# Layer 0 of a four-layer convolution stack: paired products summed in PSUM by TensorE, frame transforms dealt anew over the slots

## The chip, the cores and the metric

The kernel runs on one core of one Trainium2 chip. The metric is the device time of one execution in microseconds (us), the median of three runs where several were made.

## The reference, cut to what matters

The input x has the shape (4, 16, 512, 512): four images of sixteen frames. Four layers follow, each of the form x = x + f(groupnorm(x)). Only layer 0 is touched here:

```
def _denoise_block(x, w1, b1, w2, b2, w3, b3, a, b, c):
    trip = _triplets(x)                  # frame t with its two neighbours t-1, t+1 (mirrored at the ends)
    ...
    o = a * conv5x5(trip, w1, dilation 1) + b * conv5x5(trip, w2, dilation 2) + c * conv5x5(trip, w3, dilation 4)
    return tanh(o + biases)
y = _denoise_block(groupnorm(x), block 1)
z = _denoise_block(y, block 2)
x = x + z
```

All in float32. Layer 1 is a quantised 3x3 convolution, layer 2 a 17x17 box filter, layer 3 a product in Fourier space. They are the same in both kernels.

## The kernel before, in words

**Groups and slots.** Layer 0 runs its two blocks one after the other (`conv` 0, then `conv` 1), for 4 images each. The text calls them the first and the second convolution. Along the frame axis the three-tap sum over t-1, t, t+1 is computed for four output frames at a time out of six products in place of twelve (a short-convolution scheme, F(4,3)). Four output frames are a *group*: 4 groups an image, 16 in the first convolution (groups 0 to 15), 16 in the second (16 to 31). A group has six *slots*, p = 0 to 5, one for each product; `ORDER` says which product q runs in which slot. One slot is 144 float32 matmul instructions of TensorE (288 matmul records), 80 that write 64 output rows and 64 that write 32, all on one transformed frame `v[q]` and one set of weights `w[q]`. They write a PSUM tile `m` of 128 x 4 x 512; there are two such tiles.

**Before the products: frame transforms.** A group has six input frames d0 to d5, each a tile of 128 x 2376 (ten such tiles in a free list, `self.free`). VectorE makes from them, with one instruction of 128 x 2376 for each step, the six transformed frames: v1 and v2 from d1 to d4, v3, v4, v5 and v0. `early` does v1 and v2 (and v0) in the group before, `late` does the rest in the group's own slots 0 to 2. A group shares d0 and d1 with the group before (its d4 and d5), so it fetches four frames, one in each of the slots 0, 1, 2 and 4 of the group before (`fetch`); the first group of an image fetches five, in slots 0 to 4.
In the first convolution a frame is made from x: ScalarE normalises (L412), VectorE transposes (L445). In the second it is read from a scratch tensor y in DRAM (`y_frame`): 14 DMAs on SyncE's queue, then six small edge instructions on ScalarE (`mirror`, L484 to L488) and one small addition on VectorE (`added`, L492) in the slot after.

**After the products: gather.** In the slot after a product, `gather` takes its PSUM tile. With m1 ... the products, the four output frames are y0 = m0+m1+m2+m3+m4, y1 = (m1-m2)+2(m3-m4), y2 = (m1+m2)+4(m3+m4), y3 = (m1-m2)+8(m3-m4)+m5. Before the change ScalarE copies m1 to a tile A and m3 to C (L637); VectorE makes B = A-m2, A = A+m2, D = C-m4, C = C+m4 (L641, L642), then E = 4C+A in two halves (output frame 2), A = A+C (L648), A = A+m0 (L651), C = 2D+B, B = 8D+B, B = B+m5. ScalarE takes the tanh of each (L665 in the second convolution, L672 in the first). There is one buffer for E: the second half waits for the tanh of the first.

**What sets the order.** The whole of layer 0 stands in one order written out by hand (`slot`): each engine runs its own instructions in this order and waits on semaphores. Within a slot the order is: products; gather of the product before; tanh of A, B or C; edges; `late`; rows (the sums and extremes of finished frames: L695 and L698 on VectorE); the output (transposes `zr`, L689); the rest, in which frames are made or `added`; `early` for the next group; `fetch`. The transfers of a slot stand at its end on SyncE's queue: frames first, then the loads of x (`xb`), then the stores of finished frames (`x<-xb`); each also waits for a place in the slot's matmuls, so that they are spread over it. ScalarE also does the sums of finished frames (L714), in the same buffer as E.

**What a product waits for.** The matmuls of slot p need their transformed frame, and the PSUM tile to be free: the tile of slot p is that of slot p-2, so the gather of slot p-2, which runs during slot p-1, must be done with it.

Of the kernel before, what the change touches and what calls it, by code (L numbers as in the profile page):

```python
# [13 lines left out]
F32 = mybir.dt.float32  # L14
# [6 lines left out]
P = 128  # L21
# [7 lines left out]
PX = 32  # L29
# [6 lines left out]
ORDER = (1, 2, 3, 4, 0, 5)  # L36
# [86 lines left out]
class Layer0:  # L123
# [407 lines left out]
    def early(self, gr, step):  # L531

        nc, d, v = self.nc, gr["d"], gr["v"]
        if step == 0:
            v[1] = self.free.pop(0)
            self.stt(v[1], d[2], -4.0, d[4])
            return
        e, f = v[1], self.free.pop(0)
        self.stt(f, d[1], -4.0, d[3])
        nc.vector.tensor_add(e, e, f)  # L540
        self.stt(f, f, -2.0, e)
        v[2] = f
        if gr["g"] > 0:
            self.stt(d[0], d[0], 4.0, d[4])
            self.stt(d[0], d[2], -5.0, d[0])
            v[0] = d[0]

    def late(self, gr, p):
        nc, d, g = self.nc, gr["d"], gr["g"]
        if p == 0:  # L550
            o = d[2]
            if g == 0:
                o = gr["v"][0] = self.free.pop(0)
            nc.vector.tensor_sub(o, d[4], d[2])
            nc.vector.tensor_sub(d[1], d[3], d[1])
            gr["o"] = o
        elif p == 1:
            self.stt(d[2], d[1], 2.0, gr["o"])
            gr["v"][3] = d[2]
            if g == 3:  # L560
                self.free.append(d[4])
                nc.vector.tensor_scalar_mul(d[3], d[1], -4.0)
            else:
                nc.vector.tensor_sub(d[3], d[5], d[3])
                self.stt(d[3], d[1], -4.0, d[3])
            gr["v"][5] = d[3]
        elif p == 2:
            self.stt(d[1], d[1], -4.0, d[2])
            gr["v"][4] = d[1]


    def products(self, gr, p):
        nc, conv, q = self.nc, gr["conv"], ORDER[p]
        ps = self.psum.tile([P, 4, 512], F32, name=f"m{self.now}", tag="m")
# [15 lines left out]
        def product(at, i, weights, d, e, j, n):  # L590
            nc_ = 8 if conv else 16
            return nc.tensor.matmul(  # L592
                ps[at, i, :].rearrange("p (k c m) -> p k c m", k=nc_, c=2),
                w[PX * i : PX * i + PX, weights],
                source(i, d, e, j),
                start=(n == 0),
                stop=(n == len(order) - 1),
                skip_group_check=True,
            )
# [15 lines left out]
        gr["m"][q] = ps  # L615

    def gather(self, gr, p):

        nc, conv = self.nc, gr["conv"]
        m = gr["m"].pop(ORDER[p])  # L620
# [14 lines left out]
        if p in (0, 2):  # L635
            t = s["A" if p == 0 else "C"] = new("A" if p == 0 else "C")
            nc.scalar.copy(of(t), m)  # L637
        elif p in (1, 3):
            o, t = ("B", "A") if p == 1 else ("D", "C")
            s[o] = new(o)  # L640
            nc.vector.tensor_sub(of(s[o]), of(s[t]), m)  # L641
            nc.vector.tensor_add(of(s[t]), of(s[t]), m)  # L642
            if p == 3:
                for h in range(2):
                    e = new("E")
                    self.stt(e, s["C"][:, h], 4.0, s["A"][:, h])
                    self.activated(gr, 2, h, e)
                nc.vector.tensor_add(flat("A"), flat("A"), flat("C"))  # L648
        else:
            t = s["A" if p == 4 else "B"]  # L650
            nc.vector.tensor_add(of(t), of(t), m)  # L651
            if p == 4:
                self.stt(flat("C"), flat("D"), 2.0, flat("B"))
                self.stt(flat("B"), flat("D"), 8.0, flat("B"))
# [75 lines left out]
    def slot(self, n, p):  # L730
# [48 lines left out]
        if nxt:  # L779
            step = p - (3 if nxt["g"] == 0 else 2)  # L780
            if step in (0, 1):
                self.early(nxt, step)
            self.fetch(nxt, p)
# [1014 lines left out]
```

## Time and profile before

| | us |
|---|---|
| median of 3 runs | 5003.81 (4993.23 to 5010.5) |
| the profiled execution, device time | 5009.29 |
| its span, first to last instruction | 5007.5 |
| around the span | 1.8 |
| mean granted TensorE clock | 0.977 |
| products of layer 0 (L592), first to last | 63 to 2785 |

TensorE is busy for 94% of the span, VectorE for 80%, ScalarE for 51%. Layer 0 fills the first 2785 us. The page has a row for each engine's busy time, a chain of waits that is followed back from the last instruction, and groups of instructions by line with their mean duration; the trace behind it gives the same for any stretch. Engines are named PE (TensorE), DVE (VectorE), ACT (ScalarE), POOL (GpSimd), SP or SPq (SyncE's queue). L592 is line 592 of the kernel; L500 is a helper (`stt`) that stands for every scalar-tensor-tensor instruction of layer 0, so such rows are told apart by their tiles.

### The profile page before, as it was taken

The page shows a single profiled execution, that of the slowest core. Times are in us where ns is not written, and L with a number is a line of the kernel's source. Part 1 is how long each engine was busy: PE and PEld are TensorE (multiplying, and loading weights), DVE is VectorE, ACT ScalarE, POOL GpSimd, SP SyncE. Part 2 cuts the span into 40 slices and gives each one's busy share as a digit, 9 for nine tenths or more (in the row PEclk, how much of TensorE's full clock was granted, in tenths as well). Part 3 has the DMA queues.
Part 4 walks back from the last instruction along what each step waited for, and adds up shares of the span by engine and source line. Part 5 has one row for each costly group of instructions (what it writes and reads, how often), then busy time and mean ns, then how long its engine had stood idle before and what let it go on. Part 6 is the DMA issues. An engine that isn't in the chain of part 4 may idle for free.

```text
span 5007.5 us, 200506 instructions
## 1 busy us (share of the span) xinstructions
PE 4718.3 (94%) x90224; PEld 2669.6 (53%) x90224; DVE 4028.1 (80%) x4031; ACT 2558.2 (51%) x4156; POOL 21.4 (0%) x90
## 2 busy tenths in 40 slices
PE   4899999999999999989989699989999989999999
PEld 1344444444444444434434345548888767777776
DVE  8888888979779899899899666655555588888887
ACT  3465656563324443444434555545444456666665
POOL 0000000000000000000000000000000000000000
PEclk9999999999999999999999899999999999999999
DMA  5656665563577677776875688866666655555553
GB/s 174 167 159 168 173 167 158 154 177 99 120 143 157 151 158 158 155 161 145 163 151 134 171 267 271 266 227 228 215 215 203 208 137 148 149 143 141 152 147 115
DMA packets 393819, 850.64 MB, mean 170 GB/s; under 512 B 70912, under 2 KB 86400, under 8 KB 384512
## 3 DMA queue, kind: packets, MB, share of 16 engines
q1 hardware_dynamic: 385456, 827.22, 61.9%
q8 instruction: 707, 11.58, 1.1%
q10 hardware_dynamic: 7504, 10.60, 0.8%
q14 instruction: 152, 1.25, 0.1%
HBM read 497.51 MB, written 340.03 MB: 167 GB/s over the span
## 4 chain that ended last, share of the span: by engine, by line
PE 79%; DVE 12%; DMA 3%; issue 3%; ACT 2%; SPq 1%; ACTq 0%; POOL 0%; DVEq 0%; POOLq 0%
PE m L592 41%; PE l1p L1052 10%; PE l2p L1159 8%; PE u L1627 5%; PE s L1568 5%; PE u L1568 4%; DVE frame L500 3%; PE u L1590 2%; PE pt L1602 2%; DVE l2o L1199 2%; PE l2p L1210 1%; DVE frame L445 1%; DVE st L1200 1%; DMA frame<-y 1%; DVE B L641 1%
## 5 line engine op out<-in xcount | busy, mean ns | idle before, releaser
L592 PE MATMUL m<-frame,l0w 32*64 32x512 f32 (+1 forms) x55296 | 2609.5, 611 | 176.1 <-DVE frame L540 63.3
L592 PEld LDWEIGHTS m<-frame,l0w 32*64 32x64 f32 (+1 forms) x55296 | 1178.6, 119 | 1606.0 <-issue 1389.4
L500 DVE SCALAR_TENSOR_TENSOR frame<-frame,frame 128x2376 f32<-128x2376 f32 x232 | 607.9, 2629 | 8.6
L1052 PE MATMUL l1p<-l1q,l_wt 32*32 32x512 f32 (+1 forms) x9216 | 429.6, 604 | 48.0 <-DVE l1q L1039 41.5
L1199 DVE TENSOR_TENSOR l2o<-l2x,l2p 128x512 f32<-128x512 f32 x256 | 172.8, 675 | 263.6 <-PE l2p L1159 263.6
L714 ACT ACTIVATE junk<-xb,neg 128x1024 f32<-128x1024 f32 x256 | 294.1, 1149 | 85.4 <-issue 42.6
L1052 PEld LDWEIGHTS l1p<-l1q,l_wt 32*32 32x32 f32 (+1 forms) x9216 | 189.9, 113 | 249.8 <-issue 209.5
L1159 PEld LDWEIGHTS l2p<-k_c_band,l2y 128*128 128x128 f32 x2048 | 256.7, 190 | 75.8 <-issue 55.0
L1188 ACT COPY l2y<-l2p 128x512 f32<-128x512 f32 x256 | 150.0, 586 | 280.7 <-PE l2p L1159 280.7
L1159 PE MATMUL l2p<-k_c_band,l2y 128*128 128x144 f32 (+1 forms) x2048 | 284.2, 292 | 6.1
L445 DVE STREAM_TRANSPOSE frame<-xp 128x1056 f32<-128x1056 f32 x128 | 261.2, 2124 | 29.7 <-ACT xp L414 29.7
L1159 PE MATMUL l2p<-k_c_band,l2n 128*128 128x144 f32 (+1 forms) x2048 | 266.6, 290 | 13.8 <-DMA l2x<-x 6.8
L1159 PEld LDWEIGHTS l2p<-k_c_band,l2n 128*128 128x128 f32 x2048 | 260.1, 195 | 14.5 <-ACT l2n L1177 12.2
L1627 PE MATMUL u<-k_c_hil,zt 128*128 128x128 f32 x2048 | 255.9, 278 | 0.0
L1627 PEld LDWEIGHTS u<-k_c_hil,zt 128*128 128x128 f32 x2048 | 238.4, 192 | 2.1 <-issue 0.8
L1603 ACT COPY zt<-pt 128x512 f32<-128x512 f32 x256 | 131.4, 599 | 208.2 <-PE pt L1602 208.2
L1533 DVE TENSOR_TENSOR xc<-l3n,k_c_tab 128x2048 f32<-128x2048 f32 x64 | 146.7, 2293 | 107.6 <-ACT l3n L1517 107.6
L1067 ACT ACTIVATE l1o<-l1p,k_l_bias,l_osc 128x1024 f32<-128x1024 f32 x128 | 147.2, 1201 | 144.8 <-PE l1p L1052 139.3
L1646 DVE SCALAR_TENSOR_TENSOR l3o<-u,l3t 128x256 f32<-128x256 f32 x512 | 192.5, 427 | 22.3 <-ACT l3t L1638 19.5
L1069 DVE BATCH_NORM_STATS2 l1st<-l1o 128x6 f32<-128x512 f32 x256 | 158.2, 681 | 54.4 <-ACT l1o L1067 54.2
L1052 PE MATMUL l1p<-l1x,l_wt 32*32 32x512 f32 (+1 forms) x3064 | 195.0, 593 | 0.0
L1033 ACT ACTIVATE l1t<-l1x,l1own,l1own 128x1024 f32<-128x1024 f32 x128 | 151.8, 1234 | 81.4 <-DMA l1x<-x 76.5
(313 smaller groups left out, 6256.7 us busy)
## 6 DMA issues: line engine op xcount, KB each, us to landing
y<-y SPq DMA_DIRECT2D x256, 264.0 KB
xb<-in_x SPq DMA_DIRECT2D x512, 128.0 KB
x<-l1o SPq DMA_DIRECT2D x256, 256.0 KB
l2x<-x SPq DMA_DIRECT2D x64, 1024.0 KB
x<-l2o SPq DMA_DIRECT2D x64, 1024.0 KB
l3x<-x SPq DMA_DIRECT2D x256, 256.0 KB
out<-l3o SPq DMA_DIRECT2D x256, 256.0 KB
l1x<-x SPq DMA_DIRECT2D x252, 256.0 KB
```

The source lines that it names most:

```text
L445: nc.vector.transpose(v[:, :, :, h, 1:17].rearrange("p k u m -> p k m u"), xp)
L500: self.nc.vector.scalar_tensor_tensor(o, x, f, y, ALU.mult, ALU.add)
L592: return nc.tensor.matmul(ps[at, i, :].rearrange("p (k c m) -> p k c m", k=nc_, c=2), w[PX * i : PX * i + PX, weights], source(i, d, e, j) ...
L714: nc.scalar.activation(junk, xs[:, h], f, bias=neg, accum_out=self.out_sums[b][n][:, 2 * t + h : 2 * t + h + 1])
L1033: nc.scalar.activation(t[:, at], x[:, at], AF.Identity, bias=own[1], scale=own[0])
L1052: ins = nc.tensor.matmul(ps[at : at + hi - lo, b, :], wt[rows, d, lo:hi], qs[v % 3][rows, k, d : d + W] if d < 3 else raws[v][rows, k], st ...
L1069: nc.vector.bn_stats(st[b][:, u, :], o[:, b, :])
L1159: nc.tensor.matmul(ps[:, lo:hi], lhs[:, k, at : at + P], band[:, j : j + hi - lo], start=(k == 0), stop=(k == 3), skip_group_check=True,)
L1199: nc.vector.tensor_add(o[:, hb, :], xt[:, hb, :], ps)
L1568: nc.tensor.matmul(ps[b][32 * j : 32 * j + 32], f[rows, n, j, :], x[rows, j, :], start=(i == 0), stop=(i == 2 and tag == "s"), skip_group_ ...
L1627: nc.tensor.matmul(po[:, bass.ts(k, P)], zt[:, b, k ^ 1, :], hil[:, k, :], start=False, stop=(k == 3), skip_group_check=True,)
L1646: nc.vector.scalar_tensor_tensor(o[:, v].rearrange("p k u -> p u k"), po[:, HW:W].rearrange("p (u k) -> p u k", u=2), s, t.rearrange("p (u ...
```

## The change

In `ORDER` products 2 and 3 change places: 1, 3, 2, 4, 0, 5. A group takes two PSUM tiles for its six products and keeps them: slots 0, 2 and 4 write the first, slots 1, 3 and 5 the second. The matmuls of slots 2 (product 2), 3 (product 4) and 4 (product 0) no longer start their tile anew but add to what is in it; product 5 starts anew. So the tiles hold m1, then m1+m2, then m1+m2+m0; and m3, then m3+m4, then m5.

`gather` follows. ScalarE takes 2 m1 and 2 m3 in place of the plain copies, and two more copies, of m1+m2 (over A) and of m3+m4 (over C). VectorE takes B = A-m and D = C-m as before, reads m3+m4 for the two halves of E from PSUM in place of C, and makes A = C+m in one step in slot 4's gather. Three instructions of 128 x 2048 on VectorE go: A = A+m, C = C+m, A = A+C.

The frame transforms are the same instructions, given letters and dealt to slots by two tables, `AHEAD` (in the group before) and `SINCE` (in the group itself). The letters: a and f start v1 and v2, s finishes v1, t finishes v2; z and Z make v0; o and e are two differences; 3, u5 and 4 make v3, v5 and v4.

```diff
@@ -33,7 +33,9 @@
 ALONE = (((-4, 4), (6, 0)), ((-1, 6), (3, 5)))
 NPB = 2 * len(DELTA)
 NQ = 6
-ORDER = (1, 2, 3, 4, 0, 5)
+ORDER = (1, 3, 2, 4, 0, 5)
+AHEAD = {0: {3: "ao", 4: "fse"}, 1: ({2: "az", 3: "fs", 4: "Zoe"}, {2: "az", 3: "fstZ", 4: "oe"})}
+SINCE = {0: ({0: "3t", 1: "u5", 2: "4"}, {0: "3t", 1: "u5", 2: "4"}), 1: ({0: "3t", 1: "u5", 2: "4"}, {0: "3", 1: "u5", 2: "4"})}
 KN = 9 * 264
 NFRAMES = 10
 AFTER = mybir.DependencyInfo(mybir.DependencyClass.Sync, mybir.DependencyReason.SCHED_ONLY)
@@ -528,50 +530,62 @@
         if held is not None:
             self.free.append(held)
 
-    def early(self, gr, step):
-
-        nc, d, v = self.nc, gr["d"], gr["v"]
-        if step == 0:
-            v[1] = self.free.pop(0)
-            self.stt(v[1], d[2], -4.0, d[4])
-            return
-        e, f = v[1], self.free.pop(0)
-        self.stt(f, d[1], -4.0, d[3])
-        nc.vector.tensor_add(e, e, f)
-        self.stt(f, f, -2.0, e)
-        v[2] = f
-        if gr["g"] > 0:
-            self.stt(d[0], d[0], 4.0, d[4])
-            self.stt(d[0], d[2], -5.0, d[0])
-            v[0] = d[0]
+    def early(self, gr, p):
+        plan = AHEAD[1][gr["conv"]] if gr["g"] else AHEAD[0]
+        self.transform(gr, plan.get(p, ""))
 
     def late(self, gr, p):
-        nc, d, g = self.nc, gr["d"], gr["g"]
-        if p == 0:
-            o = d[2]
-            if g == 0:
-                o = gr["v"][0] = self.free.pop(0)
-            nc.vector.tensor_sub(o, d[4], d[2])
-            nc.vector.tensor_sub(d[1], d[3], d[1])
-            gr["o"] = o
-        elif p == 1:
-            self.stt(d[2], d[1], 2.0, gr["o"])
-            gr["v"][3] = d[2]
-            if g == 3:
-                self.free.append(d[4])
-                nc.vector.tensor_scalar_mul(d[3], d[1], -4.0)
-            else:
-                nc.vector.tensor_sub(d[3], d[5], d[3])
-                self.stt(d[3], d[1], -4.0, d[3])
-            gr["v"][5] = d[3]
-        elif p == 2:
-            self.stt(d[1], d[1], -4.0, d[2])
-            gr["v"][4] = d[1]
+        self.transform(gr, SINCE[gr["g"] > 0][gr["conv"]].get(p, ""))
+
+    def transform(self, gr, steps):
+
+        nc, d, v, g = self.nc, gr["d"], gr["v"], gr["g"]
+        for step in steps:
+            if step == "a":
+                v[1] = self.free.pop(0)
+                self.stt(v[1], d[2], -4.0, d[4])
+            elif step == "z":
+                self.stt(d[0], d[0], 4.0, d[4])
+            elif step == "Z":
+                self.stt(d[0], d[2], -5.0, d[0])
+                v[0] = d[0]
+            elif step == "f":
+                v[2] = self.free.pop(0)
+                self.stt(v[2], d[1], -4.0, d[3])
+            elif step == "s":
+                nc.vector.tensor_add(v[1], v[1], v[2])
+            elif step == "t":
+                self.stt(v[2], v[2], -2.0, v[1])
+            elif step == "o":
+                gr["o"] = d[2]
+                if g == 0:
+                    gr["o"] = v[0] = self.free.pop(0)
+                nc.vector.tensor_sub(gr["o"], d[4], d[2])
+            elif step == "e":
+                nc.vector.tensor_sub(d[1], d[3], d[1])
+            elif step == "3":
+                self.stt(d[2], d[1], 2.0, gr["o"])
+                v[3] = d[2]
+            elif step == "u":
+                if g < 3:
+                    nc.vector.tensor_sub(d[3], d[5], d[3])
+            elif step == "5":
+                if g == 3:
+                    self.free.append(d[4])
+                    nc.vector.tensor_scalar_mul(d[3], d[1], -4.0)
+                else:
+                    self.stt(d[3], d[1], -4.0, d[3])
+                v[5] = d[3]
+            elif step == "4":
+                self.stt(d[1], d[1], -4.0, d[2])
+                v[4] = d[1]
 
 
     def products(self, gr, p):
         nc, conv, q = self.nc, gr["conv"], ORDER[p]
-        ps = self.psum.tile([P, 4, 512], F32, name=f"m{self.now}", tag="m")
+        if p < 2:
+            gr["m"][p] = self.psum.tile([P, 4, 512], F32, name=f"m{self.now}", tag="m")
+        ps = gr["m"][p % 2]
         v = gr["v"][q]
         w = self.w[q]
         runs = [(e, pair) for e in range(2) for pair in PAIRS], [(e, two) for e in range(2) for two in ALONE]
@@ -593,7 +607,7 @@
                 ps[at, i, :].rearrange("p (k c m) -> p k c m", k=nc_, c=2),
                 w[PX * i : PX * i + PX, weights],
                 source(i, d, e, j),
-                start=(n == 0),
+                start=(n == 0 and q in (1, 3, 5)),
                 stop=(n == len(order) - 1),
                 skip_group_check=True,
             )
@@ -612,12 +626,11 @@
                         out = slice(64 * j + PX * u, 64 * j + PX * u + PX)
                         ins = product(out, i, slice(at, at + PX), d, e, j, n)
             self.marks.append(ins.ins)
-        gr["m"][q] = ps
 
     def gather(self, gr, p):
 
         nc, conv = self.nc, gr["conv"]
-        m = gr["m"].pop(ORDER[p])
+        m = gr["m"][p % 2]
         s = gr.setdefault("s", {})
 
         def new(tag):
@@ -632,26 +645,29 @@
         def flat(t):
             return s[t].rearrange("p h n -> p (h n)")
 
-        if p in (0, 2):
-            t = s["A" if p == 0 else "C"] = new("A" if p == 0 else "C")
-            nc.scalar.copy(of(t), m)
-        elif p in (1, 3):
-            o, t = ("B", "A") if p == 1 else ("D", "C")
-            s[o] = new(o)
-            nc.vector.tensor_sub(of(s[o]), of(s[t]), m)
-            nc.vector.tensor_add(of(s[t]), of(s[t]), m)
+        if p < 2:
+            t = s["AC"[p]] = new("AC"[p])
+            nc.scalar.mul(of(t), m, 2.0)
+        elif p < 4:
+            t = s["AC"[p - 2]]
+            o = s["BD"[p - 2]] = new("BD"[p - 2])
+            nc.vector.tensor_sub(of(o), of(t), m)
             if p == 3:
                 for h in range(2):
                     e = new("E")
-                    self.stt(e, s["C"][:, h], 4.0, s["A"][:, h])
+                    half = slice(1024 * h, 1024 * h + 1024)
+                    if conv:
+                        self.stt(e.rearrange("p (k r) -> p k r", r=PX), m[:, h], 4.0, of(s["A"])[:, h])
+                    else:
+                        self.stt(e, m[:, half], 4.0, of(s["A"])[:, half])
                     self.activated(gr, 2, h, e)
-                nc.vector.tensor_add(flat("A"), flat("A"), flat("C"))
+            nc.scalar.copy(of(t), m)
+        elif p == 4:
+            nc.vector.tensor_add(of(s["A"]), of(s["C"]), m)
+            self.stt(flat("C"), flat("D"), 2.0, flat("B"))
+            self.stt(flat("B"), flat("D"), 8.0, flat("B"))
         else:
-            t = s["A" if p == 4 else "B"]
-            nc.vector.tensor_add(of(t), of(t), m)
-            if p == 4:
-                self.stt(flat("C"), flat("D"), 2.0, flat("B"))
-                self.stt(flat("B"), flat("D"), 8.0, flat("B"))
+            nc.vector.tensor_add(of(s["B"]), of(s["B"]), m)
 
 
     def activated(self, gr, i, h, src):
@@ -777,9 +793,7 @@
         self.do("rest")
         self.do("last")
         if nxt:
-            step = p - (3 if nxt["g"] == 0 else 2)
-            if step in (0, 1):
-                self.early(nxt, step)
+            self.early(nxt, p)
             self.fetch(nxt, p)
         if cur and cur["conv"] == 0 and cur["b"] + 1 < B and p >= 2:
             self.input_stats(cur["b"] + 1, 4 * cur["g"] + p - 2)
```

## The prediction

> **What bounds the kernel now.** I read the page first: its busy times, and the chain of waits by engine.
>
> ```profile
> PE 4718.3 (94%) x90224; PEld 2669.6 (53%) x90224; DVE 4028.1 (80%) x4031; ACT 2558.2 (51%) x4156; POOL 21.4 (0%) x90
> ...
> PE 79%; DVE 12%; DMA 3%; issue 3%; ACT 2%; SPq 1%; ACTq 0%; POOL 0%; DVEq 0%; POOLq 0%
> ```
>
> TensorE bounds the program, and the DVE share of the chain is what a change could take out. Only layer 0 changes, so next come the stretches of its two convolutions.
>
> ```profile
> 63.00:1414.00 1351.00, 1297.01 (x27648) 591.53 (x27656) 1151.42 (x793) 686.74 (x1137) 18.33 (x78) 0.98 0.57 153
> 1414.00:2785.00 1371.00, 1311.90 (x27656) 587.11 (x27640) 1239.56 (x738) 581.33 (x1004) 0.37 (x2) 0.98 0.72 151
> ```
>
> (Length, then busy time of PE, PEld, DVE, ACT, POOL; granted clock, DMA share, GB/s.) Cut at the first matmul of each product, undisturbed slots last 12.8 us (p even) and 13.7 us (p odd): a group of six is 79.5 us, 32 groups are 2544 us. They take 2722 us. So 178 us in all are lost to layer 0's waits: 78 in the first convolution, 98 in the second. No version of this change can win more. VectorE, at 1240 of 1371 us, is nearly full in the second convolution, so I looked at one middle group there, group 25, slots 1 to 4:
>
> ```profile
> 2203.11:2216.80 13.69, 13.69 (x313) 6.47 (x292) 13.62 (x9) 8.31 (x16) 0.00 (x0) 1.00 0.90 167
> 2216.80:2233.50 16.70, 13.45 (x296) 5.52 (x281) 16.63 (x11) 11.54 (x21) 0.00 (x0) 0.99 0.81 184
> 2233.50:2248.37 14.87, 14.87 (x289) 6.12 (x297) 14.63 (x9) 6.36 (x14) 0.00 (x0) 0.90 0.81 190
> 2248.37:2261.21 12.84, 12.84 (x296) 5.68 (x284) 11.48 (x6) 1.15 (x1) 0.00 (x0) 1.00 0.81 169
> ```
>
> Slot 2 ends 3.25 us late, and slot 3 then costs 14.87 in place of 13.69, at a granted clock of 0.90. VectorE's timeline shows what was late:
>
> ```profile
> 2226.21 2.28 DVE L641 TENSOR_TENSOR B<-A,m 128x2048 f32<-128x2048 f32 x1
> 2228.52 2.29 DVE L642 TENSOR_TENSOR A<-A,m 128x2048 f32<-128x2048 f32 x1
> 2230.73 2.63 DVE L500 SCALAR_TENSOR_TENSOR frame<-frame,frame 128x2376 f32<-128x2376 f32 x1
> ...
> 2240.64 0.25 DVE L492 TENSOR_TENSOR frame<-frame,edge 128x72 f32<-128x72 f32 x1
> 2241.00 2.63 DVE L500 SCALAR_TENSOR_TENSOR frame<-frame,frame 128x2376 f32<-128x2376 f32 x1
> 2243.66 2.63 DVE L540 TENSOR_TENSOR frame<-frame,frame 128x2376 f32<-128x2376 f32 x1
> 2246.33 7.84 DVE L500 SCALAR_TENSOR_TENSOR frame<-frame,frame 128x2376 f32<-128x2376 f32 x3
> 2254.09 2.28 DVE L641 TENSOR_TENSOR D<-C,m 128x2048 f32<-128x2048 f32 x1
> 2256.41 2.29 DVE L642 TENSOR_TENSOR C<-C,m 128x2048 f32<-128x2048 f32 x1
> 2258.80 1.23 DVE L500 SCALAR_TENSOR_TENSOR E<-C,A 128x1024 f32<-128x1024 f32 x1
> 2261.24 1.22 DVE L500 SCALAR_TENSOR_TENSOR E<-C,A 128x1024 f32<-128x1024 f32 x1 [1.22 <-ACT z L665]
> ```
>
> v4 (2230.73) is queued behind the gather and ends as slot 3 starts. Then, in slot 3, the last frame of the next group arrives (the addition at 2240.64), five transforms follow (f, s, t, z, Z), and only then D and C, which set the PSUM tile free for slot 5. That second chain ends at 2258.70, in time for slot 5 at 2261.21. Why is the frame so late? SyncE's queue and ScalarE's wait:
>
> ```profile
> 2207.27 9.79 SPq L228 DMA_DIRECT2D frame<-y  x14
> 2217.53 4.30 SPq L228 DMA_DIRECT2D xb<-in_x  x8
> 2221.92 4.81 SPq L228 DMA_DIRECT2D x<-xb  x8
> 2226.83 8.79 SPq L228 DMA_DIRECT2D frame<-y  x14
> ```
>
> ```profile
> 2237.97 0.63 ACT L484 ACTIVATE frame<-frame,k_c_parity 128x36 f32<-128x36 f32 x2 [5.82 <-DMA frame<-y]
> ```
>
> The queue issues without a pause from slot 1 on: frame, loads, stores, frame. The edge work on the last frame starts 47.7 us after the group's slot 0. In the other middle groups (17, 18, 21, 22, 26, 29, 30) it is 51.6, 47.4, 49.6, 47.5, 46.4, 49.0, 48.9, and it does not follow the length of slot 2 (13.7 us in 22 and 30, 15 to 17 in the others). So the queue sets it, not TensorE.
>
> **The change, part by part.** *VectorE's sum.* Three instructions of 2.29 us (L642 twice, L648) go from each of 32 groups: 220 us. A middle group of the second convolution has 83 us of VectorE work now and 76 after, against 79.5. The two halves of E read PSUM in place of SBUF: no row has that form, but D<-C,m (2.28) and A<-A,C (2.29) differ by nothing, so I take nothing (-0.1 to +0.3 each). Adding in PSUM in place of starting: already 13 of the 14 steps of a slot add, so nothing.
>
> *ScalarE.* Two copies of 1.86 us (L637) and scaling in two others (nearest rows: a copy of 2048 in 1.86, two activations of 1024 in 2.3; I take 2.1) add 4.2 us to a group. ScalarE has 7.4 us of work in a slot. But the copy of m1+m2 waits for B on VectorE; behind it in the queue stand the last frame's normalising (first convolution) or edges (second). In the second it ends some 4.2 us into slot 3 (B 2.3, copy 1.9), before that frame lands; no cost. No DMA is added or moved, and SyncE's order stays.
>
> *What goes.* v4 is no longer behind B and A, and v3 moves from slot 1 to 0, so slots 2 to 3 of group 25 no longer stall: 3.25 us, and 1.2 us of half clock after it.
>
> *What is late next.* The release of the second PSUM tile. Before: D, C, release, 4.71 us from D's start to slot 5 (2170.97 to 2175.68 in group 24, where the product waits for just this). After: D 2.3, then E, tanh, E, tanh (2.44 us each pair, 2258.80 to 2261.24, since E has one buffer), then the copy of m3+m4, which stands behind both tanhs: 2.3 + 4.9 + 1.9 + 0.15 = 9.25 us. So it grows by 4.5 us. Against that the transforms between frame and D go from five to four (z is moved to slot 2): 2.6 us less. Balance: +1.9 us on the chain from the frame's landing to slot 5.
>
> Start of the edge work to slot 5: 1.5 (edges) + 0.4 + 5 x 2.62 + 4.7 = 19.7 us before. Groups 20, 24, 28 (first of an image; edge work 58.3, 57.1, 60.0 us after slot 0) start slot 5 after 78.0, 76.8, 79.6, and 29 and 30 after 68.7 and 68.5: all are edge plus 19.6 to 19.7. After: edge plus 21.6, or 65.9 (the floor) if that is more.
> - The eight middle groups: edge times sum to 388.0, plus 8 x 21.6 gives 560.8 us; they take 560.0 now. So +0.8: the stall of slot 3 comes back in front of slot 5, at 4.2 us a group.
> - It is paid with the half clock in slot 5, which now has none: 8 x 1.2 = +9.6 (the row of slot 3, 14.87 against 13.69). The 1.2 paid in slot 3 now is inside the 560.0.
> - Groups 20, 24, 28: 3 x 1.9 = +5.7. They pay the half clock already.
>
> Second convolution: +16 us. Bounds: if the frames come as much earlier as slot 2 gets shorter, its stalls go: -35. If each landing shifts 2 us later and the clock costs 2.2 (slot 3 of group 18: 15.88): +40.
>
> *First convolution.* Here ScalarE and VectorE make the frames. A plain group (5): d2 ready 2.35 us into slot 2, v4 2.6, d4 4.3, a and z 5.3: B starts 1.8 us into slot 3; B, copy, normalising (1.6), two transposes, f and s put D 3.6 us into slot 4; plus 9.25 is 12.85, and the slot lasts 12.8. No loss, no gain, but no margin. The first group of an image (4, 8, 12: 9.4 us lost each) stalls 6.55 us in front of slot 3 now. After, from u at 446.4: u5 5.2, frame 7.8, v4 2.6 (462.0, slot 3 in time), d4 4.1, a and z 5.3, B 2.3, copy 1.9, normalising and transposes 5.7, f and s 5.4, release 9.4: slot 5 at 496.1, now 497.9. The 1.8 won goes to the half clock, which moves behind the stall (15.84 against 13.7): +0.3 each. Groups 6 and 10 stay. Group 0 splits its 10.7 and 4.8 us stalls into three: +3. First convolution +4 (-12 to +12).
>
> *Sum.* 5009.3 + 16 + 4 = 5029 for the profiled execution, which lies 5.5 above the median; so 5024.
>
> [...] By the row, 3.25 us of waiting was followed by 0.90. [...]
>
> **Rivals.** *VectorE's load is the bound (faster).* 220 us less work; if frames land with the slots, the stalls of slots 2 to 4 go: -35 in the second convolution, -12 in the first: 5004 - 47 = 4957. For it: DVE 1240 of 1371, and the releaser of slot 3 is DVE in most groups. Against: the edge times.
> *The stall moves at no price (same).* As forecast, but the clock stays up over the new stalls and the landings come 1 us earlier: 5004 +- 15.
> *ScalarE's queue (much slower).* If the copies wait behind late frame edges (their DMA wait here is 5.8 us) in each second group, slot 4 waits too: 16 x 3 more, 5070.
> *Not what it says.* If adding in PSUM slowed matmuls by 1%, +27; the rows of L592 (599 and 627 ns) mix both kinds, which speaks against it.
>
> **How the numbers follow.** A run of this kernel tells 0.3% (15 us) from no change. Forecast 0.44 and ScalarE's queue 0.03 (slower), moved at no price 0.27, load 0.26. The range runs from most of the load case to the upper end of the forecast: 4960 to 5048.
>
> **What would show it.** Right: no DVE wait in front of slot 3 in the middle groups, a wait in front of slot 5 of 3 to 5 us (13 to 16 in 20, 24, 28) released by ACT's copy; edge work still 46 to 52 us after slot 0; DVE busy about 3810. Wrong: edge work at 44 or less, slot 5 without a wait, layer 0 below 2700 us; or a wait in front of slot 4.

## The result, and the profile after

The changed kernel takes 5014.02 us (median of 20 runs) where the kernel before takes 5002.45 (20 runs of it): ratio 1.0023, interval 1.0014 to 1.0032. It is slower by some 11.6 us (0.23%), a little over half of the forecast's 20. That is inside the 0.3% that the prediction took as the least that can be told; with 20 runs of each the interval lies above 1. The profiled execution after takes 5015.8 (span 5014.0), 1.8 above its median; that of before lies 6.8 above the median of 20. So the two traces differ by 6.5 where the medians differ by 11.6.

Busy times and the chain of waits, from the page:

```profile
PE 4729.7 (94%) x90224; PEld 2675.9 (53%) x90224; DVE 3807.4 (76%) x3935; ACT 2666.0 (53%) x4220; POOL 21.4 (0%) x90
...
PE 79%; DVE 12%; DMA 3%; ACT 3%; issue 2%; SPq 1%; ACTq 0%; DVEq 0%; POOL 0%; POOLq 0%
```

VectorE lost 221 us of work (4028.1 to 3807.4) and keeps its 12% of the chain. The two convolutions, in the columns used before:

```profile
63.00:1414.00 1351.00, 1304.57 (x27857) 590.71 (x27873) 1048.60 (x750) 743.79 (x1177) 18.49 (x79) 0.98 0.57 154
1414.00:2785.00 1371.00, 1307.42 (x27371) 589.00 (x27346) 1116.23 (x680) 630.70 (x1024) 0.19 (x1) 0.98 0.71 150
```

An undisturbed slot lasts 12.8 or 13.7 us in both kernels, those that add in PSUM too, to within 0.1 us; so adding there costs the matmuls nothing that can be seen. Over these, layer 0 now loses 66.1 us in the first convolution (78.0 before) and 113.5 in the second (98.5). Group 25 again, slots 1 to 5:

```profile
2197.50:2211.25 13.75, 13.75 (x314) 6.73 (x293) 13.68 (x9) 10.18 (x17) 0.00 (x0) 1.00 0.93 165
2211.25:2224.09 12.84, 12.84 (x296) 5.77 (x284) 7.65 (x7) 8.21 (x15) 0.00 (x0) 1.00 0.77 198
2224.09:2238.39 14.30, 13.88 (x314) 6.16 (x293) 10.82 (x7) 6.69 (x13) 0.00 (x0) 1.00 0.80 151
2238.39:2254.47 16.08, 13.46 (x297) 5.48 (x281) 14.77 (x9) 5.45 (x7) 0.00 (x0) 1.00 0.93 193
2254.47:2269.28 14.81, 14.81 (x288) 6.74 (x296) 14.71 (x8) 3.57 (x8) 0.00 (x0) 0.88 0.51 138
```

The stall at the end of slot 2 is gone. Slot 4 now ends late (16.08 in place of 12.84), and slot 5 behind it takes 14.81 us at a granted clock of 0.88 (0.50 from 2256.4 to 2258.4, the "half clock"). VectorE has time to spare in slots 2 and 3: 7.65 of 12.84 us, 10.82 of 14.30. Its timeline there shows what for:

```profile
2219.33 2.29 DVE L711 CUSTOM_DVE_ANT_0 xb<-xb,zr 128x2048 f32<-128x2048 f32 x1 [5.16 <-DMA x<-xb]
...
2224.22 5.18 DVE L502 SCALAR_TENSOR_TENSOR frame<-frame,frame 128x2376 f32<-128x2376 f32 x2
2229.32 2.28 DVE L654 TENSOR_TENSOR B<-A,m 128x2048 f32<-128x2048 f32 x1
2234.90 0.26 DVE L494 TENSOR_TENSOR frame<-frame,edge 128x72 f32<-128x72 f32 x1 [3.30 <-DMA x<-xb]
...
2245.63 2.28 DVE L654 TENSOR_TENSOR D<-C,m 128x2048 f32<-128x2048 f32 x1
2247.83 1.22 DVE L502 SCALAR_TENSOR_TENSOR E<-m,A 128x1024 f32<-128x1024 f32 x1
```

And ScalarE's:

```profile
2231.63 1.87 ACT L664 COPY A<-m 128x2048 f32<-128x2048 f32 x1 [11.11 <-DVE B L654]
2233.39 0.61 ACT L486 ACTIVATE frame<-frame,k_c_parity 128x36 f32<-128x36 f32 x2
...
2252.57 1.84 ACT L664 COPY C<-m 128x2048 f32<-128x2048 f32 x1
```

Read as one chain: the row of slot 2 (L711) waits 5.16 us for x; behind it stand a and z (2224.22), then B (2229.32); ScalarE waits 11.11 us for B, copies m1+m2, and does the edge work on the last frame without a pause; then f, s, t, Z, D, E, tanh, E, tanh, the copy of m3+m4, and slot 5 as that copy ends, at 2254.47. The profile names the store x<-xb as L711's releaser. What the row reads is the load of x in the same queue, issued 2212.44 to 2216.26; a run below bears that out. In the kernel before, VectorE came to this row of group 25 only 16.5 us into slot 2 and did not wait for x; now it comes to it 2.9 us into slot 2, since B and A = A+m no longer stand ahead of it and slots 0 and 1 hold one transform fewer each. The row before:

```profile
2233.27 2.28 DVE L695 CUSTOM_DVE_ANT_0 xb<-xb,zr 128x2048 f32<-128x2048 f32 x1
```

Before, the edge work waited for its frame; one line of the waits of the second convolution, before:

```profile
ACT frame L484 <- DMA frame<-y: 89.6, 23, 7.1
```

and two of those after, neither in a comparable size before (waiting engine and line, what it waited for: us in total, times, longest):

```profile
ACT A L664 <- DVE B L654: 156.7, 16, 12.7
DVE xb L711 <- DMA x<-xb: 94.0, 14, 9.9
```

VectorE's work in the stretch of the second convolution fell by 123 us (1239.6 to 1116.2; three instructions of 2.29 us in 16 groups are 110 of it), and its row now waits 103.5 us for x (94.0, and 9.5 put down to the load itself) where it waited 7.0.

### The profile page after: what moved, and what is told of

The parts are those of the page before. It is cut to its first block, busy times and chain, and to the rows that moved or that the text cites. A ratio compares the mean times of both kernels' runs of the same rounds, so it can differ in the third digit from the quotient of the medians.

```text
span 5014.0 us, 200466 instructions
## 1 busy us (share of the span) xinstructions
PE 4729.7 (94%) x90224; PEld 2675.9 (53%) x90224; DVE 3807.4 (76%) x3935; ACT 2666.0 (53%) x4220; POOL 21.4 (0%) x90
## 4 chain that ended last, share of the span: by engine, by line
PE 79%; DVE 12%; DMA 3%; ACT 3%; issue 2%; SPq 1%; ACTq 0%; DVEq 0%; POOL 0%; POOLq 0%
PE m L606 41%; PE l1p L1066 9%; PE l2p L1173 8%; PE u L1641 5%; PE s L1582 5%; PE u L1582 4%; DVE frame L502 3%; PE u L1604 2%; PE pt L1616 2%; DVE l2o L1213 2%; DVE frame L447 2%; PE l2p L1224 1%; DVE st L1214 1%; DVE frame L556 1%; DMA frame<-y 1%
## 5 line engine op out<-in xcount | busy, mean ns | idle before, releaser
L1066 PE MATMUL l1p<-l1q,l_wt 32*32 32x512 f32 (+1 forms) x9216 | 428.2, 601 | 47.0 <-DVE l1q L1053 41.5
L664 ACT COPY A<-m 128x2048 f32<-128x2048 f32 x32 | 59.7, 1867 | 312.0 <-DVE B L654 304.3
L711 DVE CUSTOM_DVE_ANT_0 xb<-xb,zr 128x2048 f32<-128x2048 f32 x64 | 146.2, 2285 | 103.6 <-DMA x<-xb 94.0
```

The lines of the kernel that those rows point to most:

```text
L1066: ins = nc.tensor.matmul(ps[at : at + hi - lo, b, :], wt[rows, d, lo:hi], qs[v % 3][rows, k, d : d + W] if d < 3 else raws[v][rows, k], st ...
```

## The experiments

Ratios are to the kernel before, run beside on the same chip. It took 5001.35 to 5013.03 us there (the row "before" is that of the main result), so the ratios are to be compared and not the medians. "Loss" is what layer 0's slots take over 12.82 and 13.70 us in one profiled execution. "Edge to slot 5" goes from the start of the edge work on the group's last fetched frame to slot 5's first matmul, where slot 5 waits for it; in each kernel it is constant within 0.03 us over these groups.

| kernel | median, us | ratio | loss, first and second convolution | edge to slot 5 |
|---|---|---|---|---|
| before | 5002.45 | 1 | 78.0, 98.5 | 19.68 |
| changed | 5014.02 | 1.0023 (1.0014 to 1.0032) | 66.1, 113.5 | 21.07 |
| redeal_only | 4986.97 | 0.9968 (0.9959 to 0.9978) | 66.7, 88.5 | 17.01 |
| psum_only | 5113.55 | 1.0221 (1.0203 to 1.0240) | 144.9, 132.3 | 23.75 |
| copy_first | 5000.33 | 0.9995 (0.9983 to 1.0006) | 65.6, 97.5 | 20.17 |
| hybrid | 4994.77 | 0.9960 (0.9947 to 0.9974) | 58.2, 101.1 | 16.89 |
| hybrid_v3 | 4985.39 | 0.9958 (0.9945 to 0.9971) | 53.0, 97.5 | 16.89 |
| stores_on_act | 5122.14 | 1.0242 (1.0222 to 1.0262) | 63.5, 220.4 | |
| frame_early | 5094.11 | 1.0160 (1.0144 to 1.0176) | 63.0, 180.2 | |
| hybrid_frame_early | 5047.08 | 1.0071 (1.0057 to 1.0085) | 54.0, 148.4 | |
| frame_mid | 5044.36 | 1.0081 (1.0068 to 1.0095) | 69.6, 135.7 | |
| frame_mid_late | 5028.05 | 1.0047 (1.0035 to 1.0059) | 64.3, 115.3 | 21.08 |
| hybrid_v3_mid | 4985.92 | 0.9965 (0.9953 to 0.9978) | 54.2, 88.7 | 16.89 |
| x_first | 5022.67 | 1.0030 (1.0015 to 1.0045) | 68.0, 109.9 | 21.08 |

### The two halves of the change

**redeal_only**: `AHEAD`, `SINCE` and `transform` of the changed kernel with the old order, products and gather.

```diff
-ORDER = (1, 3, 2, 4, 0, 5)
+ORDER = (1, 2, 3, 4, 0, 5)
...
```

> The new dealing of the frame transforms with the old order of products, the old gather and its three VectorE steps (VectorE work as before the change). If the price of the change is the longer release of the second PSUM tile, paid on a chain from the last frame's landing, then this kernel has the gain without the price: v3 leaves slot 1 for slot 0 and v4 is no longer late for slot 3, four transforms in place of five stand between the frame and D, and the release stays at 4.7 us; from edge work to slot 5 some 17.1 us in place of 19.7. But a middle group of the second convolution still has some 83 us of VectorE work for 79.5 us of products, so about 3 us a group stay. I expect 4980, ratio to before 0.991 to 0.998. If VectorE's load sets the time, as the rival has it, the dealing alone changes nothing: 5000 to 5008, ratio 1.00.

Measured 0.9968, inside the range, and edge to slot 5 17.01. Its waits in the second convolution fall to 8.8 us in front of slot 3 (18.4 before) and to 14.5 in front of slot 5 (23.6), and some new ones for VectorE stand in front of slots 0 and 1 (6.8 and 6.3). The dealing alone is a gain, with no VectorE work removed.

**psum_only**: the changed kernel with the old dealing.

```diff
+AHEAD = {0: {3: "a", 4: "fst"}, 1: ({2: "a", 3: "fstzZ"}, {2: "a", 3: "fstzZ"})}
+SINCE = {0: ({0: "oe3", 1: "u5", 2: "4"}, {0: "oe3", 1: "u5", 2: "4"}), 1: ({0: "oe3", 1: "u5", 2: "4"}, {0: "oe3", 1: "u5", 2: "4"})}
```

> The sums in PSUM with the old dealing of the transforms (all of v1, v2, v0 in slots 2 and 3 of the group before; v3 in slot 0, since product 3 now runs in slot 1). VectorE has as little work as in the changed kernel. By the release chain D stands behind one transform more in the second convolution (edge work to slot 5 some 23.7 us in place of 21.1) and behind three more in the first, less one that slot 2 no longer has; a plain group of the first convolution, which now has no margin, stalls some 5 us in front of slot 5 and pays the half clock. I expect 5060 to 5120, ratio to before 1.011 to 1.023. By the load rival it equals the changed kernel: 5014, ratio 1.002.

Measured 1.0221, inside the range, and edge to slot 5 23.75, one transform (2.68) more than the changed kernel; the first convolution loses 79 us more, with slot 4 longer by 6.1 to 6.4 us, in front of slot 5, in groups 2, 4 to 6, 8 to 10 and 12 to 14. With the same VectorE work as the changed kernel it is 100 us slower. So the rival in which VectorE's load sets the time is out for this pair: the order of its work does. The two halves don't add: on the new dealing the sums in PSUM cost 0.55% (1.0023 over 0.9968), on the old one 2.2%.

### The release of the second tile

**copy_first**: ScalarE's copy of m3+m4 right behind D.

```diff
             nc.vector.tensor_sub(of(o), of(t), m)
+            nc.scalar.copy(of(t), m)
             if p == 3:
                 for h in range(2):
                     ...
                     self.activated(gr, 2, h, e)
-            nc.scalar.copy(of(t), m)
```

> The changed kernel with one move: ScalarE copies m3+m4 out of PSUM right behind D, ahead of the two tanhs, so that its copy no longer waits for both halves of E. By the release chain the PSUM tile is free 2.3 us earlier (when the second half of E has been read, D + 2.3 + 1.9 + 1.2 + 1.2): edge work to slot 5 falls from 21.1 to 18.8 us. Groups 17, 18, 22 lose their 1 us waits, 25, 26 and 30 2.4 us of theirs and most of the half clock, 20, 24, 28 and 4, 8, 12 2.3 us each: 20 to 30 us in all, 4984 to 4994, ratio to before 0.994 to 0.999. If VectorE's load or the frames' landing alone set the time, nothing changes: 5014, ratio 1.002.

Measured 0.9995, 0.28% below the changed kernel and just outside the range; edge to slot 5 20.17, not 18.8. VectorE's timeline shows the missing 1.4 us, at D's end in group 24:

```profile
2151.28 2.28 DVE L654 TENSOR_TENSOR D<-C,m 128x2048 f32<-128x2048 f32 x1
2155.49 1.23 DVE L502 SCALAR_TENSOR_TENSOR E<-m,A 128x1024 f32<-128x1024 f32 x1 [1.93 <-ACT C L655]
2157.93 1.22 DVE L502 SCALAR_TENSOR_TENSOR E<-m,A 128x1024 f32<-128x1024 f32 x1 [1.22 <-ACT z L681]
```

The first half of E starts, at 2155.49, only as ScalarE's copy of the same PSUM tile ends (2153.59 to 2155.45), though neither writes what the other reads. Two reads that were to lie side by side became a sequence; why, no run shows.

**hybrid**: products 1, 2 and 0 are added in PSUM; product 4 starts its tile anew and C = C+m4 is VectorE's again, so that the tile is free after D and C.

```diff
-                start=(n == 0 and q in (1, 3, 5)),
+                start=(n == 0 and q in (1, 3, 4, 5)),
...
-            nc.scalar.mul(of(t), m, 2.0)
+            nc.scalar.mul(of(t), m, 2.0 - p)
...
+            if p == 2:
+                nc.scalar.copy(of(t), m)
+            else:
+                nc.vector.tensor_add(of(t), of(t), m)
+                for h in range(2):
+                    ...
+                    self.stt(e, s["C"][:, h], 4.0, s["A"][:, h])
```

> The changed kernel, but only products 1, 2 and 0 are added in PSUM; product 4 starts its tile anew, VectorE makes D = C-m4 and C = C+m4 as before the change, and E reads C from SBUF. VectorE has one step of 2.29 us more in a group than in the changed kernel, two less than before the change. By the release chain the second tile is free after D and C, 4.7 us after D starts (8.84 in the changed kernel), so edge work to slot 5 is 17.0 us: with edge work at 48 to 51 us slot 5 no longer waits in groups 17, 18, 22, 25, 26, 30, groups 20, 24, 28 and 4, 8, 12 wait some 4 us less: 30 to 45 us off the changed kernel, 4969 to 4984, ratio to before 0.993 to 0.997, faster than the new dealing alone (0.9968) or equal to it. If less VectorE work were what gives the time, it would lie between the changed kernel and the kernel before: 5002 to 5014.

Measured 0.9960, inside the range, and edge to slot 5 16.89. VectorE has 32 steps of 2.29 us, some 73 us, more work than in the changed kernel, and the time is 0.6% less. So the longer release is what the sums in PSUM cost on the new dealing. The waits in front of slot 5 in the second convolution fall from 30.1 us to 5.6. But 21.8 us now stand in front of slot 1, where there were none: v3, which product 3's new place wants a slot earlier, is late. Against redeal_only (0.9968) the intervals overlap: that the sums in PSUM which are left gain anything over the new dealing alone is not shown.

**hybrid_v3**: hybrid with v3 a slot earlier, ahead of the rows (the edit is against hybrid).

```diff
-AHEAD = {0: {3: "ao", 4: "fse"}, 1: ({2: "az", 3: "fs", 4: "Zoe"}, {2: "az", 3: "fstZ", 4: "oe"})}
-SINCE = {0: ({0: "3t", 1: "u5", 2: "4"}, {0: "3t", 1: "u5", 2: "4"}), 1: ({0: "3t", 1: "u5", 2: "4"}, {0: "3", 1: "u5", 2: "4"})}
+AHEAD = {0: {3: "ao", 4: "fse"}, 1: ({2: "az", 3: "fs", 4: "Zoe", 5: "3"}, {2: "az", 3: "fstZ", 4: "oe", 5: "3"})}
+SINCE = {0: ({0: "3t", 1: "u5", 2: "4"}, {0: "3t", 1: "u5", 2: "4"}), 1: ({0: "t", 1: "u5", 2: "4"}, {1: "u5", 2: "4"})}
...
             self.late(cur, p)
+        if nxt and p == 5:
+            self.early(nxt, p)
         self.do("rows")
...
         if nxt:
-            self.early(nxt, p)
+            if p < 5:
+                self.early(nxt, p)
```

> The kernel that adds products 1, 2 and 0 alone in PSUM, with v3 of groups 1 to 3 of an image made in slot 5 of the group before, ahead of that slot's rows and transposes, in place of slot 0: product 3 now runs in slot 1, and in that kernel VectorE worked without a pause from D to v3, which then was 3.4 us late for slot 1 (groups 21, 23, 25, 27, 29, 31: 5.6, 4.2, 5.7, 5.7, 3.2, 4.7 us lost; 2.3 to 2.5 in 5, 9, 13). If the lateness is one of order on VectorE, these go: 25 to 35 us, 4960 to 4970, ratio to before 0.989 to 0.993. If it is VectorE's load, the wait turns up in a later slot and the time stays at 4985 to 4995, ratio 0.995 to 0.997.

Measured 0.9958, as expected if VectorE's load holds it; its interval overlaps hybrid's. The waits in front of slot 1 fall only to 11.6 us: it is now B+m5, which has to free slot 5's tile, that is 2.8 us late in 21, 25 and 29. From D on VectorE works there without a pause but the 1.2 us between the halves of E; what is put ahead of one deadline is late for the next. So here its load does count, locally.

### The landing

**stores_on_act** moves the 32 stores of a group to ScalarE's queue.

```diff
-move = nc.scalar.dma_start if self.last_groups else partial(self.move, what="stores")
+move = nc.scalar.dma_start
```

> The changed kernel with the stores of finished frames in the second convolution issued from ScalarE's queue in place of SyncE's. If SyncE's queue sets when the last frame lands, its transfers of slots 1 and 2 stand some 4.8 us earlier: edge work 43 to 46 us after slot 0 in the middle groups in place of 48 to 51, and the waits in front of slot 5 go in groups 17, 18, 22, 25, 26, 30: 15 to 20 us, 4995, ratio to before 0.997 to 1.000, less what ScalarE pays for issuing (32 stores of about 0.6 us a group, which may delay its copies). If the transfers themselves, not the queue, set the landing, edge work stays at 48 to 51 us and the time is 5014 or above.

Measured 1.0242, a miss: edge work is later (53 to 58 us in the middle groups), so this doesn't tell queue from transfer. SyncE's queue is held at its head: 11 loads of x from 2224.76 took it 28.86 us, with the frames behind them. The reading is that stores issued in ScalarE's order come late and so x's three buffers come free late; no run shows that step by itself.

**frame_early** fetches d3 in slot 1 behind d4, ahead of the loads; its edge work moves to slot 2 with it. **hybrid_frame_early** is the same in hybrid.

```diff
-            order = {0: (2,), 1: (4,), 2: (3,), 4: (5,)}
+            order = {0: (2,), 1: (4, 3), 4: (5,)} if conv else {0: (2,), 1: (4,), 2: (3,), 4: (5,)}
```

> The changed kernel, with the last frame (d3) of the second convolution's groups 1 to 3 of an image fetched in slot 1 right behind d4, ahead of that slot's loads and stores, in place of slot 2. If SyncE's queue sets when it lands, edge work on it starts some 36 to 40 us after the group's slot 0 in place of 48 to 51, f, s, t and Z start right behind B, and the waits in front of slot 5 go in groups 17, 18, 22, 25, 26, 30 and shrink in 20, 24, 28: 20 to 35 us, 4980 to 4994, ratio to before 0.996 to 0.999. If the chain from the frame is not what slot 5 waits for (the release alone is, by ScalarE's queue), the waits stay: 5014, ratio 1.002.

> Both: products 1, 2 and 0 added in PSUM, product 4 not, and the last frame fetched in slot 1. If the release and the landing are two ends of one chain, the second adds little to the first in the middle groups (their waits are gone by either) and only groups 20, 24, 28 gain more: 0 to 15 us below the better of the two, ratio to before 0.990 to 0.996.

The frame does land as the queue has it: edge work at 38.9 to 42.5 us in the middle groups. But the times are 1.0160 and 1.0071, both misses. In frame_early the row (L711) now waits 215 us for x, whose loads moved back by some 10 us, and a, z, B and D stand behind it.

**frame_mid** puts d3 behind slot 1's loads and ahead of its stores; **frame_mid_late** also keeps the edge work in slot 3.

```diff
-        moves = [m for what in ("first", "loads", "stores") for m in self.moves[what]]
+        moves = [m for what in ("first", "loads", "mid", "stores") for m in self.moves[what]]
...
-            order = {0: (2,), 1: (4,), 2: (3,), 4: (5,)}
+            order = {0: (2,), 1: (4, 3), 4: (5,)} if conv else {0: (2,), 1: (4,), 2: (3,), 4: (5,)}
...
-                gr["d"][i] = self.y_frame(gr, i, t)
+                gr["d"][i] = self.y_frame(gr, i, t, "mid" if p == 1 and i == 3 else "first")
...
-        self.later(1, mirror, "edges")
-        self.later(1, added)
+        self.later(2 if what == "mid" else 1, mirror, "edges")
+        self.later(2 if what == "mid" else 1, added)
```

(The last two lines are frame_mid_late's; in frame_mid both stay at 1.)

> The changed kernel, with the last frame (d3) of groups 1 to 3 of an image in the second convolution fetched in slot 1, behind that slot's loads of x and ahead of its stores (in place of slot 2; in the kernel with the frame ahead of both, its edge work started 40 us after slot 0, but the loads came 10 us later and VectorE waited for them). If SyncE's queue is full, so that each transfer brought forward puts another back, then the frame lands some 4.8 us earlier (edge work 43 to 46 us after slot 0) and slot 5 no longer waits in 17, 18, 22, 25, 26, 30, while the stores are late by some 9 us; x has three buffers, so the next loads may wait for them. Without that: 4994 to 5004, ratio to before 0.996 to 0.999; with it, waits of DVE for x and 5020 to 5050. A frame that does not land earlier would speak against the queue: 5014.

> As the kernel with the last frame fetched between loads and stores of slot 1, but the edge work on it stays in slot 3. (In that kernel the frame landed earlier, 42.6 to 45.6 us after slot 0, but its edge work, now in slot 2, stood ahead of a, z and B on VectorE, so these waited for it: 19.4 us from edge work to D in place of 12.2.) If the chain from landing to slot 5 sets the time, the edge work now starts 43 to 46 us after slot 0 with 21.1 us behind it, so slot 5 waits nowhere in 17, 18, 22, 25, 26, 30 (64 to 67 against 65.9): 15 to 30 us below the changed kernel, 4985 to 5000, ratio to before 0.996 to 0.999. If the later stores take it back (x waits for a buffer, VectorE's rows for x), 5010 or above.

In frame_mid edge work starts at 42.6 to 45.6 us, as expected of the queue, but in slot 2 it stands ahead of a, z and B on VectorE: 19.4 us to D in place of 12.2, 1.0081. In frame_mid_late the edge work is back at 48 to 51 us, with the frame there some 4 us earlier: ScalarE is never idle in front of it, the copy of m1+m2 is what ends. VectorE's row waits 114 us for DMAs (103.5 in the changed kernel), and the time is 1.0047. This is the run that broke the prediction's reason: in the changed kernel it is no longer the frame that the edge work waits for.

**x_first** is frame_mid_late with the order loads, d4, d3, stores in slot 1.

```diff
-        moves = [m for what in ("first", "loads", "mid", "stores") for m in self.moves[what]]
+        kinds = ("loads", "first", "mid", "stores") if self.moves["mid"] else ("first", "loads", "stores")
+        moves = [m for what in kinds for m in self.moves[what]]
```

> As the kernel with the last frame fetched behind slot 1's loads and its edge work kept in slot 3, but with the loads of x first in slot 1, ahead of d4 (so: loads, d4, d3, stores). That kernel showed that in the middle groups the edge work no longer waits for the frame: ScalarE's copy of m1+m2 stands in front of it and waits for B, B for a and z, and these, on VectorE, stand behind the row of slot 2 (L711), which waits for x (94 us in all in the changed kernel, 2 before the change). If so, with x 10 us earlier L711 waits less than 30 us in all, B starts 40 to 42 us after slot 0 in the middle groups (44 to 46 now), the edge work at 44 to 46 (48 to 51), and slot 5 waits nowhere in 17, 18, 22, 25, 26, 30: 10 to 25 us below the changed kernel, 4989 to 5004, ratio to before 0.997 to 1.000. If VectorE's load sets B, it stays at 44 to 46 and the time at 5014 or above; the stores, behind both frames, may take some of it back by holding x's buffers.

The chain moves the way expected, if less far: the row waits 53 us for x in place of 103.5 (under 30 expected), B starts at 41.9 to 43.6 us in the middle groups (43.6 to 46.4 in the changed kernel), edge work at 46.0 to 47.6 (47.7 to 51.2), and in front of slot 5 nothing is left in 17, 18, 22, 25, 26, 29 and 30 (0.7 us in 21); so the load of x held the chain. The time does not follow: 1.0030, not to be told from the changed kernel. In the trace, most of what was won in waits (44.0 to 28.7 us over all slots of the second convolution) is lost inside the slots, as told below; whether the new order of transfers makes these losses, one trace doesn't show.

**hybrid_v3_mid**: frame_mid_late's transfers in hybrid_v3.

> The same transfer order in the kernel that adds only products 1, 2 and 0 in PSUM and makes v3 in slot 5. There the waits that were left (2.8 us in front of slot 1, for B+m5 on VectorE, in 21, 25, 29, 31) come from D being late, and D from the frame; if so they go too: 4960 to 4975, ratio to before 0.991 to 0.994. If VectorE's load holds them, 4985, ratio 0.996.

Measured 0.9965, its interval overlapping hybrid_v3's: the transfers give nothing that can be told here either.

## Why the prediction was right, and where it was not

*Right: the stall moves.* In front of slot 3 the second convolution waited 18.4 us before and 0.0 now; in front of slot 5 23.6 and now 30.1, with ScalarE's copy as releaser. The second convolution was put at +16 and is at +15.1, though by misses that cancel, as told below.

*Right: the chain behind the edge work.* 21.6 us forecast, 21.07 measured in all nine groups that wait for it, and 23.75, 17.01 and 16.89 where a part was undone: one transform more, four transforms with the old release, four with hybrid's. The release is 8.84 us in place of 9.25; the sum took durations end to end, where the next instruction starts up to 0.1 us before the end of the one ahead.

*Wrong: what the edge work waits for.* "In the second it ends some 4.2 us into slot 3 ... before that frame lands; no cost" is the step that failed. The copy of m1+m2 ends 9.4 us into slot 3 in group 25, since B starts 5.2 us into it: a and z now stand ahead of B, and the row ahead of them waits for x. The text saw a full queue and drew from it only the frame; the same queue carries x, and VectorE now comes to the row before the load has landed. That the edge work still starts 47.7 to 51.2 us after slot 0, as the text had it (46 to 52), is luck, a coincidence of two chains: it was the frame before, it is the copy now (no idle time of ScalarE in front of it in 11 of 12 groups of the second convolution; 2.3 to 9.7 us before). The signs named did not tell the two apart; ScalarE's releaser in front of the edge work would have. So does the sum over the eight middle groups agree by luck: edge work is 4.2 us later in all, the chain 4.2 us shorter, and the two give the 560.8 us of the forecast; slot 5 in fact starts after 565.1, since a stall inside slot 3 holds up group 29. What the failed step costs the middle groups in time stays open: in x_first the wait for x was halved and the time stayed.

*Wrong in the same place: groups 20, 24, 28.* A wait in front of slot 4 (7.28, 1.86, 4.77 us), released by the copy of m1+m2, was named as a sign against the forecast, and it came; slot 5 waits 4.4 to 5.9 and not 13 to 16. These three lose 50.6 us in place of 41.5: +9.1 against +5.7. The wait in front of slot 4 is a cost of the same step: there too B stands behind a, z and the row.

*Mis-sized: the half clock.* 8 x 1.2 was put on the middle groups. Waits of 1.07, 1.14 and 0.81 us (17, 18, 22) cost none; those of 2.62, 3.28 and 5.22 (25, 26, 30) were followed by a clock of 0.88, 0.88 and 0.86 and cost 1.1, 1.1 and 1.4. Groups 21 and 29 do not wait in front of slot 5 at all, so the sign of 3 to 5 us in the middle groups came true in 26 and, about, in 25 and 30. The eight lose 42.2 in place of 37.5: +4.7 against +10.4. The other five groups, where nothing was forecast, lose 1.3 more. The misses cancel. The rows show no one length of waiting that decides: in the kernel before, a wait of 1.92 us (group 2) was followed by a clock of 0.89 and one of 1.97 us (group 29) by the full clock.

*Mis-sized: the first convolution.* +4 was put on it; it is -12.0. "Groups 6 and 10 stay" failed: they lost 3.7 us each and now 0.3 and 0.4, and group 2 went from 4.1 to 0.5. Their two small stalls (v4 late for slot 3, then C for slot 5) were the mechanism of the second convolution, and went with it; they were left as they were without being worked out. Group 0, put at +3, is at -2.4. Groups 4, 8 and 12 are as forecast in sum (27.9 to 27.8 us), but with a wait of 1.5 to 1.6 us in front of slot 1, for a frame transform, that the forecast did not have.

*Small slips.* ScalarE's work in a slot, put at 7.4 us, is 6.5 in group 25 (39.19 us over its six slots), and the change adds 3.4 us to a group (107.8 over 32) where 4.2 was put; nothing rests on either.

*The sum.* In the slots +15.1 - 12.0 = +3.1; with 1.3 us at the start and 2.0 behind layer 0, that is the 6.5 of the two traces, to rounding. The rest of the 11.6 between the medians lies in how the two profiled executions stand to their medians, and no trace divides it.

*The rivals.* VectorE's load as the bound was wrong for this change (psum_only, hybrid), but it counts in places: in hybrid_v3 it holds slot 1. "The stall moves at no price" came as near as the forecast (5004 and 5024; measured 5014). ScalarE's queue has its share, not as priced: slot 4 does wait, 13.9 us in all in 20, 24 and 28, but because the copy waits for B, not for the frames. Slower matmuls are out: the undisturbed slots last 12.8 and 13.7 us, as before.

## What to carry to other kernels

When an engine is relieved, ask for each of its instructions what it would wait for if it came earlier; where a queue is full, every transfer in it is such a candidate, not only the one that is late now. A constant from one event to another, over all groups that wait, tells which chain binds; but look at what releases its first event before and after, because two chains can put it at the same time. Take a change apart, keep the part that shortens the chain and leave the part that lengthens a release: the new dealing alone gives 0.9968 in place of 1.0023. With sums in PSUM only for the tile that is not awaited it is 0.9960 and 0.9958, not to be told from the dealing alone.

## What the runs showed of the hardware

**Stalls inside a slot.** Some slots lose time with nothing to wait for that the profile shows ("issue"). In x_first's group 25, slot 3, on TensorE:

```profile
2234.03 6.49 PE L607 MATMUL m<-frame,l0w 32*32 32x512 f32 x63 [3.50 <-issue]
```

and the DMA queues of that kernel, first from 2226.6 to 2231 us, then from 2231 to 2236.5 (packets, MB, share of 16 engines):

```profile
q1 hardware_dynamic: 226, 0.52, 96.4%
```

```profile
q1 hardware_dynamic: 515, 0.80, 59.8%
q8 instruction: 2, 0.03, 3.1%
```

The stall runs from 2230.5 to 2234.0. In the 4.4 us up to 2231 the DMA engines were busy with data for 96.4%, and no packet of the instruction queue moved. In the trace of the changed kernel each of the 15 such stalls of over 0.3 us in the second convolution ends 2.9 to 3.7 us after a 16 KB packet of the instruction queue began. In the 4 us ahead of each of these 15 packets the DMA engines were over 90% busy; 217 such packets began in that stretch, and of the 202 without a stall 74 came behind engines as busy. So busy engines went with every stall there and did not make one alone. These stalls were 19.2 us there (16.9 before, 30.2 in x_first), and the slots that hold them, with the lower clock behind them (0.83 over slot 3 of group 25 in x_first), lose 40 us (33, 54): nearly as much as all the waits in front of slots there (44.0). What makes these stalls is not shown; no run took the data away.

**Two readers of one PSUM tile.** In copy_first VectorE's read began 0.04 us after ScalarE's read of the same tile had ended, 1.93 us after VectorE was ready for it. It cost that run 1.4 of the 2.3 us it was made for.
